# Selective scan: adding sixteen state terms by accumulating transfers into two SBUF sums

## The chip, the cores and the metric

The kernel runs on one core of one Trainium2 chip. The metric is the device time of one execution in microseconds (us). The kernel before takes 5587.63 us, the median of three runs between 5581.73 and 5599.81 us. The profiled execution that this text reads has a span of 5600.4 us. Shares, waits and instants below are of that execution.

## The reference

The program is two layers on an input of 4 images, 128 channels and 64x64 pixels. The first layer is a convolution block with a Mamba (selective scan) branch, the second is attention with 4 heads and a mixture of 8 experts. Only the scan is touched:

```python
dA = jnp.exp(delta[..., None] * A)
dBu = delta[..., None] * Bm[:, :, None, :] * xin[..., None]
def step(h, inp):
    dA_t, dBu_t, C_t = inp
    h = dA_t * h + dBu_t
    y = jnp.einsum('bdn,bn->bd', h, C_t)
    return (h, y)
...
y = jnp.transpose(ys, (1, 0, 2)) + D_skip * xin
out = y * jax.nn.silu(z) @ out_proj_w.T
```

There are N = 16 states for each channel. The einsum is a sum over the 16 states of h times C. It is this sum whose adding changes hands.

## The kernel before

The sequence of each image (4096 positions) is cut into 8 blocks of 512. Channels lie on the 128 partitions, in two halves p = 0 and 1 for each block. One **unit** of the scan is one image, one block, one half and one state: 4 x 8 x 2 x 16 = 1024 units, in that order, one for each turn of the main loop at L1207, called a slot. A unit does the following:

- `fetched` (L732) loads `rows`, B and C of that state broadcast to the partitions, 512 KB, three slots ahead. The pool has four buffers.
- `decayed` (L742) makes `da` = exp(delta x A) on ScalarE, two slots ahead.
- `scan` (L747) runs three VectorE instructions on 128x512 float32: `h` = rows x du, then the scan itself (TENSOR_TENSOR_SCAN, in place in `h`), then `hc` = rows x h, the term of that state. `hc` has 5 buffers (L756).
- ScalarE copies the last column of `h` to `state`, in the next slot.

For the first 128 units (`ALONE`, L1204), when there is no attention to run yet, every term is added by TensorE: a matmul of `hc` with the identity into the PSUM tile `y`. From unit 128 on, GpSimd adds the terms of an even and an odd state in SBUF (L1232), and TensorE adds the eight pair sums into `y` (L1241), two slots later. After the sixteenth state `scanned` (L760) does xin = xin x dsk + y on VectorE, reading PSUM, and zs = xin x zs on GpSimd.

Everything else is woven into the same slots, by two devices. **Attention** is a generator (L894): each slot takes one group, which is four `sc` matmuls, two exponentials `pT` on ScalarE and, a slot later, eight `av` matmul records (`weighted`, L950). Two **lanes**, X and Y, hold generators of stages (group norm, first norm, convolution, the scan's `inputs`, `closed`, and the attention's `finished` with the experts); each half slot moves a lane by one stage. The lanes' layer norms (`normalised`, L502) have a chain of four small GpSimd instructions, `rs` and `shift`, whose result ScalarE needs for `xt` two stages later.

All instructions go through the wrapper at L445, which ties each to the one before it on the same engine. So the order on every engine's queue is the order of this Python text, and an instruction that waits holds back all that are behind it on its engine. For the same reason nearly every row of the profile has line L445, and the tiles' names tell the operations apart. Loads and stores are all issued by SyncE, in one queue.

When the units are used up, near 4976 us, attention groups and the experts remain, up to the end.

Of the kernel before, what the change touches and what calls it, by code (L numbers as in the profile page):

```python
# [9 lines left out]
F32 = mybir.dt.float32  # L10
# [3 lines left out]
ALU = mybir.AluOpType  # L14
# [3 lines left out]
P = 128  # L18
C = 128
EPS = 1e-5  # L20
BLK = 512
# [3 lines left out]
NST = 16  # L25
# [11 lines left out]
def conv_mamba_attn_moe_kernel(ctx: ExitStack, tc: tile.TileContext, t: dict):  # L37
    nc = tc.nc
    x, out = t["x"], t["out"]
# [13 lines left out]
    def load(name, shape=None, src=None, eng=nc.sync, pool=const):  # L53
        src = t[name] if src is None else src
        w = pool.tile(list(shape or src.shape), F32, name=f"w_{name}")
        eng.dma_start(out=w, in_=src)
        return w

    ident = const.tile([P, P], F32, name="ident")
# [13 lines left out]
    inz, cb, dtb, dsk, wbc = (load(k) for k in ("inz", "cb", "dtb", "dsk", "wbc"))  # L73
# [365 lines left out]
    class Queue:  # L439
# [7 lines left out]
    tensor, vector, scalar, gpsimd, sync = (  # L447
        Queue(e) for e in (nc.tensor, nc.vector, nc.scalar, nc.gpsimd, nc.sync)
    )

    def mm(out, lhsT, rhs, start=True, stop=True):
        tensor.matmul(out, lhsT=lhsT, rhs=rhs, start=start, stop=stop)
# [11 lines left out]
    def flush():  # L464
        for entry in outgoing:
            entry[0] -= 1
            if entry[0] == 0:
                sync.dma_start(out=entry[1], in_=entry[2])
        outgoing[:] = [entry for entry in outgoing if entry[0]]
# [7 lines left out]
    def pool(name, bufs=1, space=None):  # L477
        return main.enter_context(
            tc.tile_pool(name=name, bufs=bufs, **({} if space is None else {"space": space}))
        )  # L480

    mix, att, side = pool("mix"), pool("att"), pool("side")
# [48 lines left out]
    group_of, y0_of, xn_of, pairs_of, in_of, gated, kqv = {}, {}, {}, {}, {}, {}, {}  # L531
# [200 lines left out]
    def fetched(b, i, p, n):  # L732

        bcd = in_of[b, i, p][4]
        w = mix.tile([P, 2, BLK], F32, name="rows", bufs=4)
        sync.dma_start(
            out=w.rearrange("p k q -> p (k q)"),
            in_=bcd[:, n, :][None].to_broadcast([DI, 2, 2 * BLK]),
        )
        return w  # L740

    def decayed(b, i, p, n):  # L742
        da = mix.tile([P, BLK], F32, name="da", bufs=3)
        scalar.activation(da, in_of[b, i, p][2], AF.Exp, scale=amat[:, n : n + 1])
        return da

    def scan(b, i, p, n, w, da):  # L747

        du = in_of[b, i, p][3]
        h = mix.tile([P, BLK], F32, name="h", bufs=3)  # L750
        vector.tensor_mul(h, w[:, 0, :], du)
        vector.tensor_tensor_scan(
            out=h, data0=da, data1=h, initial=0.0 if i == 0 else states[b % 2][:, p, n : n + 1],
            op0=ALU.mult, op1=ALU.add,
        )
        hc = mix.tile([P, BLK], F32, name="hc", bufs=5)  # L756
        vector.tensor_mul(hc, w[:, 1, :], h)
        return h, hc

    def scanned(b, i, p, y):  # L760
        xin, zs, delta, du, bcd = in_of.pop((b, i, p))
        vector.scalar_tensor_tensor(xin, xin, dsk, y, ALU.mult, ALU.add)
        gpsimd.tensor_mul(zs, xin, zs)
        gated[b, i, p] = zs

# [184 lines left out]
    def weighted(group):  # L950
        b, q, h, pTs, first, last, prev, final = group
        if first:
            sums[0] = ps_av.tile([P, BLK], F32, name="av")
        av = sums[0]
        for k, (v, pT) in enumerate(pTs):
            for u in range(2):
                mm(
                    av[64 * u : 64 * u + 2 * DH, :], v, pT[:, u, :],
                    first and k == 0, last and k == STEP - 1,
                )  # L960
        if last:
            avs = att.tile([P, BLK], F32, name="avs", bufs=2)
            scalar.copy(avs, av)
            if prev is not None:
                gpsimd.tensor_add(avs, avs, prev)


            if not final:
                partial[b, q, h] = dram.tile([P, BLK], F32, name=f"avd{q}{h}")
                send(partial[b, q, h], avs, 3)  # L970
                return
            if h == 0:
                total[b, q] = dram.tile([2, 2, NH, DH, BLK], F32, name=f"total{q}")
            d = total[b, q]
            send(d[:, :, h].rearrange("u k r q -> (u k) r q"), avs, 3)
            if h == NH - 1:
                work_left = inverted(b, q)
                later.extend((slot + n, work_left) for n in (4, 6, 8))
# [148 lines left out]
    def advance(lane, second):  # L1127

        if inside[lane] != second:
            return False  # L1130
        while True:
            if lane not in running:

                tasks = lanes[lane] if lanes[lane] or slot < len(units) else lanes["X"]
                if not tasks or not all(k in done for k in tasks[0][2]):
                    return False
                key, stages, _ = tasks.popleft()
                running[lane] = key, stages(lane) if callable(stages) else stages
            key, stages = running[lane]
            try:  # L1140
                next(stages)
                inside[lane] = not second
                return True
            except StopIteration:
                assert not second
                done.add(key)
                del running[lane]

    def until(key):
        while key not in done:  # L1150
            flush()
            count = len(done)
            moved = [
                advance(*half) for half in (("X", True), ("Y", False), ("Y", True), ("X", False))
            ]
            assert any(moved) or len(done) > count, key
# [17 lines left out]
    for k in range(-2, len(blocks)):  # L1174
        if 0 <= k:
            b, i = blocks[k]
            Y.append((("in", b, i, 1), inputs(b, i, 1), [("scan", *blocks[k - 1], 1)] if k else []))
        if k + 2 < len(blocks):
            b, i = blocks[k + 2]
            if k + 2 == 0 or i > 0:  # L1180
                upper(k + 2)
        if 0 <= k + 1 < len(blocks):
            b, i = blocks[k + 1]
# [20 lines left out]
    ALONE = NB // 2 * 2 * NST  # L1204
    rows, decays, old, due = {}, {}, None, deque()
    even, y_of, waiting, slot = None, {}, None, 0
    while slot < len(units) or due or waiting or left or later or lanes["X"] or running:  # L1207
        flush()

        for ahead in range(slot if slot == 0 else slot + 3, min(slot + 4, len(units))):  # L1210
            until(("in", *units[ahead][:3]))
            rows[ahead] = fetched(*units[ahead])
        if old:
            (b, i, p, n), h = old
            if i < NB - 1:
                scalar.copy(states[b % 2][:, p, n : n + 1], h[:, BLK - 1 : BLK])
            old = None
        for ahead in range(slot if slot == 0 else slot + 2, min(slot + 3, len(units))):
            decays[ahead] = decayed(*units[ahead])
        group = next(groups, None)  # L1220
        if slot < len(units):
            unit = units[slot]
            h, hc = scan(*unit, rows.pop(slot), decays.pop(slot))
            old = unit, h
            b, i, p, n = unit

            if slot < ALONE:
                due.append((slot + 1, unit, hc, n == 0))
            elif n % 2 == 0:
                even = hc  # L1230
            else:
                gpsimd.tensor_add(even, even, hc)  # L1232
                due.append((slot + 2, unit, even, n == 1))
        advance("X", True)
        advance("Y", False)
        while due and due[0][0] <= slot:
            _, unit, term, first = due.popleft()
            b, i, p, n = unit
            if first:
                y_of[b, i, p] = ps_y.tile([P, BLK], F32, name="y")  # L1240
            mm(y_of[b, i, p], ident, term, first, n == NST - 1)  # L1241
            if n == NST - 1:
                scanned(b, i, p, y_of.pop((b, i, p)))
                done.add(("scan", b, i, p))
                if p == 1:
                    lanes["X"].appendleft((("closed", b, i), closed(b, i), []))
        advance("Y", True)
        if waiting:
            weighted(waiting)
        waiting = group  # L1250
        advance("X", False)
        while later and later[0][0] <= slot:
            next(later.popleft()[1])
        slot += 1
# [6 lines left out]
    with tc.If(nc.values_load(general[0:1, 0:1]) > 0):  # L1261
# [4 lines left out]
        with tc.For_i(0, B, 1) as b:  # L1266
# [3 lines left out]
                out=t_tok.rearrange("p k c -> p (k c)"),  # L1270
                in_=tsave[bass.ds(b, 1)].rearrange("o p q -> (o p) q"),
# [96 lines left out]
```

## Time and profile before

A row is a stretch of the profiled run, with the busy time of each engine as a share of the stretch. The DMA share is the mean busy share of the 16 DMA engines.

| stretch, us | what runs | TensorE | VectorE | ScalarE | GpSimd | DMA |
|---|---|---|---|---|---|---|
| 560 to 4976 | units 128 to 1023, attention, both lanes | 91% | 82% | 75% | 44% | 63% |
| 4976 to 5600 | rest of attention, experts | 92% | 19% | 54% | 7% | 38% |

The first 560 us hold the 128 units without pairing. Instruction times that matter: the pair addition on GpSimd has a mean of 1465 ns (448 of them), a matmul record of `y` 662 ns (1152 of them, two for each matmul), the scan 1464 ns, the two products on VectorE 811 and 783 ns.

How to read it: a busy share says how much room an engine has over the stretch, not which engine sets the pace at an instant. That needs the chain of waits and the timeline, since each engine executes strictly in its own order.

### The profile page before, as it was taken

To read this page: it belongs to the slowest core of one execution; us is meant where nothing else is said; L and a number is where in the kernel's file an instruction comes from. 1 tells how busy PE (TensorE), PEld (TensorE's weight loads), DVE (VectorE), ACT (ScalarE), POOL (GpSimd) and SP (SyncE) were. 2 spreads that over 40 slices of the span, in tenths; PEclk is the share of its full clock that TensorE was granted. 3 is DMA by queue.
4 is the path that set the end of the run, shared out by engine and by line. 5 is a ranking of instruction groups with operands and counts; after the bars stand their busy time and mean duration, and the time that the engine had idled before them with its cause. 6 is when DMAs were issued, how large, how long until landed. Compare 5 with 4: busy or idle time off the path is not lost.

```text
span 5600.4 us, 60586 instructions
## 1 busy us (share of the span) xinstructions
PE 4916.5 (88%) x17866; PEld 2040.8 (36%) x17866; DVE 4174.5 (75%) x6275; ACT 3892.2 (69%) x5957; POOL 2161.8 (39%) x1885
## 2 busy tenths in 40 slices
PE   4666798988999988999998899898999989899997
PEld 2222333333333333333333333333333333344343
DVE  4888877887888888887887888887888888741221
ACT  3455587787777777787777777687777777666553
POOL 2333444454444444445443444444444443320000
PEclk7777799999999999999999999999999999999998
DMA  3455566666666666667665556666765666654432
GB/s 95 169 171 176 194 210 210 205 228 211 230 208 203 210 208 216 205 225 229 224 211 192 192 200 213 219 221 209 232 223 202 206 205 209 210 183 154 147 121 67
DMA packets 427635, 1097.91 MB, mean 196 GB/s; under 512 B 48401, under 2 KB 131746, under 8 KB 427298
## 3 DMA queue, kind: packets, MB, share of 16 engines
q1 hardware_dynamic: 426130, 1093.17, 58.5%
q8 instruction: 144, 2.36, 0.2%
q14 instruction: 193, 1.58, 0.1%
q10 hardware_dynamic: 1168, 0.80, 0.1%
HBM read 941.95 MB, written 135.00 MB: 192 GB/s over the span
## 4 chain that ended last, share of the span: by engine, by line
PE 45%; DVE 21%; ACT 15%; issue 7%; POOL 6%; DMA 5%; SPq 1%; DVEq 0%; ACTq 0%; POOLq 0%
PE av L445 17%; DVE h L445 11%; PE sc L445 10%; PE ps_X L445 8%; PE ps_Y L445 5%; ACT pT L445 5%; PE y L445 4%; ACT L445 3%; ACT xt L445 3%; DVE hc L445 2%; DVE cm L445 2%; POOL rsY L445 1%; POOL rsX L445 1%; DMA ks<-kd 1%; ACT da L445 1%
## 5 line engine op out<-in xcount | busy, mean ns | idle before, releaser
L445 ACT ACTIVATE pT<-sc 128x1024 f32<-128x1024 f32 x2048 | 1983.7, 1022 | 1017.6 <-PE sc L445 1015.2
L445 PE MATMUL av<-pT,v 128*64 128x512 f32 x8192 | 2004.9, 610 | 3.5 <-ACT avs L445 3.3
L445 DVE TENSOR_TENSOR_SCAN h<-da,state,h 128x512 f32<-128x512 f32 x896 | 1311.3, 1464 | 118.6 <-ACT da L445 26.8
L445 PE MATMUL sc<-qs,ks 128*128 128x512 f32 x4096 | 1308.8, 440 | 96.9 <-DMA ks<-kd 51.9
L445 POOL TENSOR_TENSOR hc<-hc 128x512 f32<-128x512 f32 x448 | 655.8, 1465 | 1718.7 <-DVE hc L445 1513.3
L445 PEld LDWEIGHTS sc<-qs,ks 128*128 128x128 f32 x4096 | 717.7, 193 | 773.7 <-ACT pT L445 283.0
L445 PEld LDWEIGHTS av<-pT,v 128*64 128x64 f32 x8192 | 501.6, 137 | 1193.3 <-issue 1105.8
L445 DVE TENSOR_TENSOR h<-rows,du 128x512 f32<-128x512 f32 x1024 | 830.6, 811 | 88.0 <-ACT state L445 38.1
L445 DVE TENSOR_TENSOR hc<-rows,h 128x512 f32<-128x512 f32 x1024 | 802.2, 783 | 78.3 <-DVE h L445 2.3
L445 ACT ACTIVATE da<-delta,amat 128x512 f32<-128x512 f32 x1024 | 749.4, 732 | 9.4 <-DVE h L445 5.2
L445 PE MATMUL y<-hc,ident 128*128 128x512 f32 x1152 | 661.5, 662 | 62.4 <-DVE hc L445 51.3
L445 ACT ACT_TABLE_LOAD x319 | 409.3, 1283 | 22.9 <-PE ps_Y L445 17.8
L445 ACT COPY state<-h 128x1 f32<-128x1 f32 x896 | 175.7, 196 | 194.8 <-DVE h L445 194.3
L445 PEld LDWEIGHTS y<-hc,ident 128*128 128x128 f32 x1152 | 219.6, 209 | 213.8 <-DVE hc L445 101.4
L445 POOL TENSOR_SCALAR rsY<-mvY 128x4 f32<-128x4 f32 x99 | 57.5, 581 | 527.3 <-DVE mvY L445 523.2
L445 POOL TENSOR_TENSOR avs<-avs,prev 128x512 f32<-128x512 f32 x64 | 89.3, 1396 | 438.1 <-ACT avs L445 319.7
L445 PE MATMUL ps_X<-share,w_ew 128*128 128x512 f32 x448 | 223.9, 622 | 20.5 <-DVE share L445 20.2
L445 ACT ACTIVATE xt<-ps_Y,shiftY,rsY 128x128 f32<-128x128 f32 x380 | 143.2, 462 | 129.9 <-POOL shiftY L445 122.4
L445 POOL TENSOR_SCALAR du<-e 128x512 f32<-128x512 f32 x64 | 145.9, 2280 | 217.2 <-ACT e L445 217.2
L445 DVE TENSOR_TENSOR share<-share,xf 128x1024 f32<-128x1024 f32 x128 | 182.8, 1428 | 51.1 <-DMA share<-sharesY 31.0
L445 DVE RECIPROCAL den<-den 128x32 f32<-128x32 f32 x16 | 5.5, 346 | 265.6 <-DMA den<-total 265.6
L445 DVE TENSOR_TENSOR_SCAN h<-da,h 128x512 f32<-128x512 f32 x128 | 182.9, 1429 | 17.3 <-ACT da L445 4.4
(234 smaller groups left out, 4729.6 us busy)
## 6 DMA issues: line engine op xcount, KB each, us to landing
rows<-bcd SPq DMA_DIRECT2D x1024, 512.0 KB
ks<-kd SPq DMA_DIRECT2D x256, 512.0 KB
qs<-qd SPq DMA_DIRECT2D x129, 512.0 KB
v<-vd SPq DMA_DIRECT2D x256, 256.0 KB
share<-sharesX SPq DMA_DIRECT2D x112, 512.0 KB
pairs<-xn SPq DMA_DIRECT2D x128, 128.5 KB
qd<-hi SPq DMA_DIRECT2D x32, 512.0 KB
qd<-lo SPq DMA_DIRECT2D x32, 512.0 KB
```

Of the source, the lines that this page charges most:

```text
L445: return lambda *args, **kw: queued(op(*args, **kw))
```

## The change

From unit 128 on, the terms of states 0 and 1 are written directly to two SBUF tiles, `ysum0` (2 buffers) and `ysum1` (1 buffer). The terms of states 2 to 15 go to `hc` (now 3 buffers) and are added to one of the two tiles by a DMA that GpSimd issues with `accum_op=ALU.add`. Even states and state 15 go to `ysum0`, odd states from 3 to 13 to `ysum1`. After state 15 VectorE folds `ysum1` in with xin x dsk + ysum1, and two slots later adds `ysum0`. The change is meant to free GpSimd and TensorE of the adding. The 128 units of the start stay as they were.

```diff
-        hc = mix.tile([P, BLK], F32, name="hc", bufs=5)
+        if slot >= ALONE and n < 2:
+            hc = mix.tile([P, BLK], F32, name=f"ysum{n}", bufs=2 - n)
+        else:
+            hc = mix.tile([P, BLK], F32, name="hc", bufs=3)
         vector.tensor_mul(hc, w[:, 1, :], h)
...
-        vector.scalar_tensor_tensor(xin, xin, dsk, y, ALU.mult, ALU.add)
+        if isinstance(y, list):
+            vector.tensor_add(xin, xin, y[0])
+        else:
+            vector.scalar_tensor_tensor(xin, xin, dsk, y, ALU.mult, ALU.add)
         gpsimd.tensor_mul(zs, xin, zs)
...
-            elif n % 2 == 0:
-                even = hc
+            elif n < 2:
+                y_of.setdefault((b, i, p), []).append(hc)
             else:
-                gpsimd.tensor_add(even, even, hc)
-                due.append((slot + 2, unit, even, n == 1))
+                to = y_of[b, i, p][n % 2 if n < NST - 1 else 0]
+                gpsimd.dma_start(out=to, in_=hc, accum_op=ALU.add)
+                if n == NST - 1:
+                    xin = in_of[b, i, p][0]
+                    vector.scalar_tensor_tensor(
+                        xin, xin, dsk, y_of[b, i, p][1], ALU.mult, ALU.add
+                    )
+                    due.append((slot + 2, unit, None, False))
...
-            mm(y_of[b, i, p], ident, term, first, n == NST - 1)
+            if term is not None:
+                mm(y_of[b, i, p], ident, term, first, n == NST - 1)
```

## The prediction

> **What bounds the kernel now.** I read the chain of waits first: its summary by engine names no single limit.
>
> ```profile
> PE 45%; DVE 21%; ACT 15%; issue 7%; POOL 6%; DMA 5%; SPq 1%; DVEq 0%; ACTq 0%; POOLq 0%
> ```
>
> TensorE carries less than half of the chain, and VectorE and ScalarE a third. Next, busy time from 560 to 4976 us, the stretch that the change touches (columns: stretch, length, busy us of TensorE, weight loads, VectorE, ScalarE, GpSimd, then clock, DMA share, GB/s).
>
> ```profile
> 560.00:4976.00 4416.00, 3998.62 (x14826) 1658.84 (x14826) 3640.45 (x5280) 3299.82 (x5072) 1940.76 (x1637) 0.96 0.63 212
> ```
>
> TensorE is busy 91% and VectorE 82%; the DMA engines have 37% left. The 624 us after it and the 560 us before it run the same instructions after the change. Third, the timeline of plain slots, in which no lane adds work (start, duration, engine, operation).
>
> ```profile
> 2402.60 1.19 PE L445 MATMUL sc<-qs,ks 128*128 128x512 f32 x4
> 2403.63 1.02 PE L445 MATMUL y<-hc,ident 128*128 128x512 f32 x2
> 2404.58 1.94 PE L445 MATMUL av<-pT,v 128*64 128x512 f32 x8
> 2406.45 1.19 PE L445 MATMUL sc<-qs,ks 128*128 128x512 f32 x4
> 2407.57 1.94 PE L445 MATMUL av<-pT,v 128*64 128x512 f32 x8
> 2409.44 1.20 PE L445 MATMUL sc<-qs,ks 128*128 128x512 f32 x4
> ```
>
> TensorE runs without a gap. A slot with a `y` matmul lasts 3.85 us (2402.60 to 2406.45), one without it 2.99 us (to 2409.44): the matmul costs 0.86 us. VectorE in the same place, with the GpSimd addition:
>
> ```profile
> 2406.55 1.28 DVE L445 TENSOR_TENSOR_SCAN h<-da,state,h 128x512 f32<-128x512 f32 x1
> 2407.94 0.69 DVE L445 TENSOR_TENSOR hc<-rows,h 128x512 f32<-128x512 f32 x1
> 2408.55 0.69 DVE L445 TENSOR_TENSOR h<-rows,du 128x512 f32<-128x512 f32 x1
> 2409.34 2.13 DVE L445 TENSOR_TENSOR_SCAN h<-da,state,h 128x512 f32<-128x512 f32 x1
> ...
> 2408.71 1.68 POOL L445 TENSOR_TENSOR hc<-hc 128x512 f32<-128x512 f32 x1 [4.74 <-DVE hc L445]
> ```
>
> The scan takes 1.28 us alone and 2.13 us when it comes up while GpSimd adds. So the addition, on an engine that is 44% busy, costs VectorE up to 0.85 us in every second slot.
>
> [...]
>
> **The change part by part.** In 896 units there are 896/16 = 56 sums, with 14 accumulating transfers each: 784 of 256 KB.
>
> *TensorE.* 448 `y` matmuls go: 448 x 0.86 = 385 us, the ceiling of the gain where TensorE sets the pace. On the chain, asked for 600 to 4976 us alone, `PE y` has 4.6%: 0.046 x 4376 = 201 us.
>
> *VectorE.* 448 GpSimd additions go. At most each releases 0.85 us: 381 us. For the lower end: by the tile views the medians of scan, first and second product are 1284, 684 and 692 ns against means of 1464, 811 and 783 ns, so collisions with all of GpSimd cost 896 x 0.180 + 1024 x 0.127 + 1024 x 0.091 = 384 us; the additions are 653 of GpSimd's 1941 us in this stretch, which gives 0.34 x 384 = 130 us. I take 230 us. VectorE is a fifth of the chain, 927 us, so 230/3640 of that is 58 us on the path. Added are 56 `tensor_add` of 0.69 us, 39 us, a fifth of it on the path: 8 us. The fold with dsk moves two slots ahead and reads SBUF; it costs what it did.
>
> *Mechanism alone:* 201 + 58 - 8 = about 250 us.
>
> *GpSimd.* It loses 656 us of additions and issues 784 transfers. An issue costs 0.52 us on SyncE (the median of the `rows` issues)[...]. I take 1 us: 784 us, about what goes, so its load stays as it is. Its queue is what matters: each transfer waits for `hc` and for the previous transfer into the same sum, two slots back (at state 15, one slot back). Behind it stand the `rs` and `shift` chain, for which ScalarE's `xt` waits with `pT` queued behind that, and `du`, `delta` and `zs`. VectorE's `hc` waits for the transfer three back (3 buffers).
>
> *Latency L of one transfer, from issue to landing.* [...] High end: a 256 KB load on SyncE's queue, `inv`, took 9.49 us on the chain at 1368 us with other loads ahead of it. The transfers have a queue of their own beside SyncE's[...]. I take 6 us. What does L do? From the timeline I took the starts of all GpSimd pair additions: 440 gaps, mean 9.96, median 9.5, a quarter under 7.55 us. Take 0.86 us off every gap and let none be under L: the sum of the changes is -369 us at L = 4, -307 at 6, -200 at 7, -45 at 8, +165 at 9, +298 at 9.5, +442 at 10. So L = 6 takes back 369 - 307 = 62 us, and the change breaks even near 8.2 us.
>
> *DMA engines.* By the queue table 1093.17 MB take 58.5% of 5600 us, 3276 us: 256 KB are 0.79 us of all 16 engines. With one read the transfers add 784 x 0.79 = 616 us, with two 1232 us, to 0.63 x 4416 = 2782 us: a share of 77 to 91%. Loads come later then. Waits on loads are now 5% of the chain, 220 us in this stretch; I let them grow by a quarter, 55 us.
>
> *Sum:* -250 + 62 + 55 = -133 us, so 5588 - 133 = 5455; I say **5460 us**. Costed at nothing: freed PSUM use, and the wait of VectorE for `y` (71 us in this stretch), which the wait for state 15's transfer replaces. That one ends 2L = 12 us after state 14's product and is needed three slots (14.8 us at 4.93 each) after it.
>
> **The rivals.**
> - *Cheap transfers.* One read and L under 5 us: the stretch gains nearly the whole mechanism, 250 us: 5340 us. For it: 37% of the DMA engines is idle. [...]
> - *A wash.* DMA delays eat the gain: 5590 us.
> - *The DMA engines become the bound.* With two reads, 2782 + 1232 = 4014 us of work; if they reach 89% at most, the stretch lasts 4510 us, 94 longer: 5680 us. For it: SyncE's loads come in bursts (five behind each other at 1368 us), and a wait for `ks` stops TensorE and ScalarE together. Against: the loads are issued two to three slots ahead.
> - *The chain of transfers is the bound.* L of 9.5 us: +298, so 5885 us; slower than before. For it: the 9.49 us seen. Against: that load stood behind others in its own queue.
>
> **How the numbers follow.** Forecast 0.44, cheap transfers 0.13, wash 0.08, DMA engines 0.18, chain of transfers 0.17. Faster 0.57, same 0.08, slower 0.35. The range of 5300 to 5850 us reaches past cheap transfers and the DMA bound, and holds of the last rival what lies under L = 9.4; about 0.17 is left out.
>
> **What would show it.** In the changed kernel's profile: `y` matmuls near 256 records instead of 1152; slots without lane work near 3.0 us in the timeline; the scan's mean down from 1464 towards 1350 ns; GpSimd waiting on DMA for little; DMA share 0.75 to 0.9 with waits for `ks` and `rows` under twice theirs. The forecast is wrong if `xt` or `hc` waits long for GpSimd or for the transfers (L over 8 us), or if TensorE idles on `ks`.

## The result, and the profile after

The changed kernel takes 5774.87 us, the median of four runs (5763.86 to 5780.07); the kernel before took 5589.66 us beside it. The ratio is 1.0328 (95% interval 1.0303 to 1.0352): 3.3% slower, where 5460 us had been forecast. Since the comparison with each experiment has runs of the kernel before on the same chip, whose medians lie between 5589 and 5593 us, medians are compared directly below, and each verdict has its ratio. The runs of one kernel spread over 10 to 40 us, so a single difference of 20 us or less between two medians says little.

The loss lies in the stretch that the change touches. Same columns as before, from 560 us to the last unit of the scan:

```profile
560.00:5128.00 4568.00, 3758.78 (x13869) 1551.27 (x13869) 3488.02 (x5323) 3291.47 (x5057) 1916.28 (x1967) 0.91 0.87 248
```

The last `rows` load is issued at 5127.9 us instead of 4954.1, so the stretch has grown by 174 us, although up to these instants TensorE (first busy column) is busy 218 us less than before (3976.7 us then) and VectorE (third) 141 us less (3628.5). The DMA share rose from 0.63 to 0.87. TensorE's granted clock fell from 0.96 to 0.91. The page's chain, its queues and the transfers' row:

```profile
q1 hardware_dynamic: 426130, 1093.17, 57.1%
q0 software_dynamic: 112896, 205.57, 20.0%
...
PE 31%; DVE 21%; DMA 18%; ACT 13%; POOL 8%; issue 7%; SPq 1%; DVEq 0%; POOLq 0%; ACTq 0%
...
L445 POOL DMA_DIRECT2D ysum<-hc x784 | 694.7, 896 | 2072.2 <-DVE hc L445 1051.9
...
ysum<-hc POOLq DMA_DIRECT2D x784, 256.0 KB, 7.0
```

The chain went from TensorE (45% to 31%) to DMA (5% to 18%). `q0` is the new queue: 205.57 MB cost a fifth of the 16 engines, while `q1` moves five times the bytes for 57.1%. An issue occupies GpSimd for 896 ns on average, so 784 of them take 694.7 us, and a transfer lands 7.0 us after its issue (last column, the median). The waits say who pays (engine and tile, what it waited for: us in total, times, longest):

```profile
POOL ysum L445 <- DMA ysum<-hc: 495.0, 128, 9.5
ACT xt L445 <- POOL shiftY L445: 186.2, 70, 24.6
DVE xin L445 <- DMA ysum<-hc: 149.0, 53, 10.0
PE sc L445 <- DMA ks<-kd: 89.9, 16, 16.6
DVE h L445 <- DMA rows<-bcd: 68.9, 31, 7.1
```

GpSimd waits 495 us for the previous transfer into the same sum, VectorE 149 us at the folds. ScalarE's `xt` waits 186.2 us for GpSimd's `shiftY` instead of 122.4. But loads that have nothing to do with the sums are waited for longer too: `ks` 89.9 us against 51.9 before, `rows` 68.9 against 20.1. Which of these sets the time can't be read from totals of waits. That is what the experiments are for.

### The profile page after: what moved, and what is told of

Its sections match the earlier page's. It is cut to its first block, busy times and chain, and to the rows that moved or that the text cites. A ratio compares the mean times of both kernels' runs of the same rounds, so it can differ in the third digit from the quotient of the medians.

```text
span 5778.0 us, 59802 instructions
## 1 busy us (share of the span) xinstructions
PE 4694.6 (81%) x16970; PEld 1941.2 (34%) x16970; DVE 4034.7 (70%) x6331; ACT 3896.3 (67%) x5957; POOL 2143.3 (37%) x2221
## 3 DMA queue, kind: packets, MB, share of 16 engines
q1 hardware_dynamic: 426130, 1093.17, 57.1%
q0 software_dynamic: 112896, 205.57, 20.0%
## 4 chain that ended last, share of the span: by engine, by line
PE 31%; DVE 21%; DMA 18%; ACT 13%; POOL 8%; issue 7%; SPq 1%; DVEq 0%; POOLq 0%; ACTq 0%
PE av L445 11%; DVE h L445 11%; DMA ysum<-hc 8%; PE ps_X L445 7%; PE sc L445 7%; PE ps_Y L445 5%; ACT pT L445 4%; ACT xt L445 2%; ACT L445 2%; DMA inv<-inverse 2%; POOL rsY L445 2%; DVE hc L445 2%; POOL rsX L445 2%; DVE cm L445 2%; DMA pairs<-xn 2%
## 5 line engine op out<-in xcount | busy, mean ns | idle before, releaser
L445 PE MATMUL av<-pT,v 128*64 128x512 f32 x8192 | 2082.6, 631 | 8.6 <-ACT avs L445 8.5
L445 PE MATMUL sc<-qs,ks 128*128 128x512 f32 x4096 | 1348.7, 451 | 164.6 <-DMA ks<-kd 89.9
L445 POOL DMA_DIRECT2D ysum<-hc x784 | 694.7, 896 | 2072.2 <-DVE hc L445 1051.9
L445 DVE TENSOR_TENSOR_SCAN h<-da,state,h 128x512 f32<-128x512 f32 x896 | 1235.6, 1379 | 118.3 <-ACT da L445 25.9
L445 DVE TENSOR_TENSOR h<-rows,du 128x512 f32<-128x512 f32 x1024 | 810.4, 791 | 132.5 <-DMA rows<-bcd 68.9
L445 DVE TENSOR_TENSOR hc<-rows,h 128x512 f32<-128x512 f32 x912 | 705.2, 773 | 98.5 <-DMA ysum<-hc 61.9
L445 ACT ACTIVATE xt<-ps_Y,shiftY,rsY 128x128 f32<-128x128 f32 x380 | 143.2, 459 | 194.3 <-POOL shiftY L445 186.2
L445 PE MATMUL ps_X<-ident,xt 128*128 128x128 f32 x372 | 105.7, 349 | 194.2 <-ACT xt L445 182.4
L445 POOL TENSOR_TENSOR zs<-xin,zs 128x512 f32<-128x512 f32 x64 | 105.4, 1646 | 327.1 <-DVE xin L445 327.1
L445 PE MATMUL y<-hc,ident 128*128 128x512 f32 x256 | 176.2, 792 | 51.3 <-DVE hc L445 51.3
L445 PE MATMUL ps_Y<-ident,xt 128*128 128x128 f32 x396 | 82.6, 343 | 157.7 <-ACT xt L445 157.3
L445 PE MATMUL ps_Y<-pairs,inxc 128*128 128x512 f32 x256 | 147.1, 704 | 63.1 <-DMA pairs<-xn 57.8
```

Source lines behind the costliest of these rows:

```text
L445: return lambda *args, **kw: queued(op(*args, **kw))
```

## The experiments

Two theories stood at the start. **Latency:** engines wait for transfers to land. **Load:** the transfers fill the DMA engines and everybody's loads come late. A third possibility was that taking the adders off is worth less than thought.

### No transfers at all

```diff
-                gpsimd.dma_start(out=to, in_=hc, accum_op=ALU.add)
```

> The changed kernel without its 784 accumulating transfers: the terms of states 2 to 15 are computed but left out of the sums, everything else stays. It measures what taking the adding off GpSimd and TensorE is worth when nothing replaces it. Theory of latency (engines wait for the landing of transfers) and theory of load (the transfers fill the DMA engines and SyncE's loads come late) both expect the whole mechanism of the prediction, some 250 us under the kernel before: 5340 us, 5280 to 5400. A theory that the mechanism itself is small (other engines take over at once) expects 5500 us or more.

Measured: 5424.89 us, ratio 0.9699 (0.9678 to 0.9720). The mechanism is worth 166 us, two thirds of the forecast's 250, and the transfers with all that hangs on them cost 5775 - 5425 = 350 us.

### The same load, with nobody waiting

```diff
+    spare = [mix.tile([P, BLK], F32, name=f"spare{k}") for k in range(3)]
...
-                to = y_of[b, i, p][n % 2 if n < NST - 1 else 0]
+                to = spare[n % 3]
...
-                        xin, xin, dsk, y_of[b, i, p][1], ALU.mult, ALU.add
+                        xin, xin, dsk, fixed, ALU.mult, ALU.add
```

The terms of states 0 and 1 go to `hc` here, like the others, and the second fold reads `fixed` (a constant tile) too.

> The same 784 accumulating transfers of 256 KB, issued at the same places, but into three rotating spare tiles that nobody reads, so that each waits for the transfer three slots back instead of two or one, and the folds on VectorE read a constant tile and wait for no transfer (the terms of all states are left out of the sums). DMA load and issue stay as in the changed kernel. Theory of load: about as slow as the changed kernel, 5700 to 5780 us, DMA share 0.87. Theory of latency: close to the kernel without transfers, 5340 to 5420 us.

Measured: 5668.29 us, ratio 1.0126 (1.0104 to 1.0148). Of the 350 us, 243 remain when no fold waits for a transfer and no transfer waits for a recent one. So waiting for the sums isn't the whole cost, and load isn't either: it leaves 107 us unexplained. The 243 us aren't load alone. They hold the issues on GpSimd, which are measured further below, and VectorE still waits 46.3 us at `hc` for the transfer three back, because `hc` has three buffers. Three rows of its waits for loads:

```profile
DVE h L445 <- DMA rows<-bcd: 113.1, 38, 8.4
PE sc L445 <- DMA ks<-kd: 108.2, 17, 16.2
PE ps_Y L445 <- DMA pairs<-xn: 72.7, 21, 11.4
```

All three are loads of SyncE's queue; without transfers these waits are 37.2, 58.2 and 30.2 us. Nothing in this kernel ties the loads to the sums, so the shared DMA engines, of which the two queues take 58.3% and 20.3% here, are the likely reason. This is argued: no view here gives the landing time of each load.

### Half the bytes, and plain copies

```diff
-                gpsimd.dma_start(out=to, in_=hc, accum_op=ALU.add)
+                gpsimd.dma_start(out=to[:, 0 : BLK // 2], in_=hc[:, 0 : BLK // 2], accum_op=ALU.add)
```

> The changed kernel with transfers of columns 0 to 255 only (128 KB instead of 256 KB; the other half of each term is left out of the sums). Number of issues and all waits stay. Both theories expect a gain; load: about half of what the transfers cost, near 5550 us, DMA share about 0.76, transfers landing in some 5 us instead of 7.0. Latency: more than half, since 5 us is under the two slots of most pairs: 5450 us or less.

Measured: 5626.03 us, ratio 1.0054 (1.0037 to 1.0071). Both expectations missed. 5550 us fit a kernel without transfers at 5340 us, as it was expected then; with the measured 5425 us, half of the cost recovered would be 5600 us. Half the bytes recover 149 of the 350 us, a little under half. These transfers land in 5.8 us, against 7.0 at full width and some 5 expected. The tiny transfers below show better that a part of the cost goes with the number of transfers and not with their size.

```diff
-                gpsimd.dma_start(out=to, in_=hc, accum_op=ALU.add)
+                gpsimd.dma_start(out=to, in_=hc)
```

> The changed kernel with plain copies in place of accumulating transfers: same bytes written, same queue, same waits, but the old sum isn't read (the sums then hold only the last term). If accumulating makes a transfer dear by its second read, the software queue falls from 20% of the DMA engines to about 10%, the landing from 7.0 to 5 to 6 us, and the time to near that of the half-width transfers, 5550 us. If a 2 KB row from GpSimd's queue is dear in any case, it stays at 5750 us and 20%.

Measured: 5591.22 us, ratio 1.0002 (0.9987 to 1.0017), 184 us under the changed kernel. The rows of the queue, of the issues and of the transfers in this kernel, in turn:

```profile
q0 software_dynamic: 62720, 205.57, 9.4%
...
L445 POOL DMA_DIRECT2D ysum<-hc x784 | 439.8, 561 | 2026.7 <-DVE hc L445 1363.9
...
ysum<-hc POOLq DMA_DIRECT2D x784, 256.0 KB, 5.4
```

The same 205.57 MB take 9.4% of the engines instead of 20.0%, with 62720 packets instead of 112896, which is 64 fewer for each transfer, and land in 5.4 us instead of 7.0. The issue on GpSimd also fell, from 896 to 561 ns. So accumulating doubles the time that a transfer takes of the DMA engines, as the forecast's upper end had it. Queue and landing are as the first branch expected, the time is 41 us above it. The 184 us are the price of accumulating as a whole: shorter issues and shorter waits at the folds (70.6 us) are in it, beside the load.

### Tiny transfers, with and without the folds' wait

```diff
-                gpsimd.dma_start(out=to, in_=hc, accum_op=ALU.add)
+                gpsimd.dma_start(out=to[:, 0:8], in_=hc[:, 0:8], accum_op=ALU.add)
```

> The changed kernel with transfers of 8 columns (4 KB in all; the other 504 columns of each term are left out of the sums). 784 issues on GpSimd and every wait stay; hardly any load is left. If load explains what the transfers cost (243 of 350 us by the three rotating tiles), this lands near the kernel without transfers, 5425 us plus the issues: 5440 to 5490 us. If the count of transfers, their issue on GpSimd and the waits on a landing[...] matter most, 5530 us or more.

Measured: 5525.41 us, ratio 0.9870 (0.9849 to 0.9892). With 4 KB for each transfer 100 of the 350 us remain. The next kernel has the same transfers and folds that read the constant tile:

> The 8-column transfers with the two folds on VectorE reading a constant tile (the scan's output leaves out all terms from unit 128 on). It splits the 100 us between no transfers (5425) and 8-column transfers (5525). If VectorE's wait at the folds is the cost, 5450 us; if it is the 784 issues of 0.9 us on GpSimd, which hold back rs and shift and with them ScalarE's xt, 5510 us.

Measured: 5506.26 us, ratio 0.9845 (0.9828 to 0.9861). Only 19 us of the 100 are the folds' wait; 81 us stay with transfers that hardly carry anything and that VectorE's folds ignore. The tiny transfers' time to landing, from the answer for their tile:

```profile
DMA to landing us min/median/max: 2.0/4.7/9.3
```

Even 4 KB take 4.7 us in the median, beside a fastest of 2.0 us. The same 4 KB can land in 2.0 us, so more than half of the median is waiting of some kind; what it waits for isn't shown.

### What the issues on GpSimd cost

The 81 us had been costed at nothing. Two kernels without transfers put something else in their place:

```diff
-                gpsimd.dma_start(out=to, in_=hc, accum_op=ALU.add)
+                gpsimd.memset(spare, 0.0)
+                gpsimd.memset(spare, 0.0)
```

> The kernel without transfers (the terms of states 2 to 15 left out of the sums) with two memsets of a spare 128x512 tile on GpSimd in the place of each transfer, some 0.4 to 0.5 us each, that wait for no other engine; hc has 2 buffers. If the time that GpSimd is occupied by the issues is their cost, 5500 us, as with tiny transfers that nobody waits for (5506). If it is the wait for hc or the transfers themselves, 5430 us.

Measured: 5465.14 us, ratio 0.9770 (0.9753 to 0.9787): 40 us over the kernel without transfers. The second kernel waits, but does little:

```diff
-                gpsimd.dma_start(out=to, in_=hc, accum_op=ALU.add)
+                gpsimd.tensor_copy(spare, hc[:, 0:1])
```

> The kernel without transfers (the terms of states 2 to 15 left out of the sums) with a GpSimd copy of one column of hc in the place of each transfer: GpSimd's queue waits for every hc as in the changed kernel, but is occupied for a short time only. If the wait in the in-order queue holds back rs and shift, 5490 us or more. If occupation is the cost, 5430 to 5445 us.

Measured: 5441.53 us, ratio 0.9719 (0.9694 to 0.9743): 17 us, of the size of the interval. The rows of the two replacements, in turn:

```profile
L445 POOL MEMSET spare<- 128x512 f32 x1568 | 824.8, 526 | 71.9
```

```profile
L445 POOL COPY spare<-hc 128x1 f32<-128x1 f32 x784 | 317.1, 405 | 1845.5 <-DVE hc L445 1818.8
```

At 526 ns each the memsets kept GpSimd busy longer than the issues would (824.8 us against 694 us) and cost half of the 81 us. The copies occupy GpSimd too, for 317.1 us, so the two experiments overlap: occupation and the in-order wait for `hc` explain at most 57 of the 81 us. The rest is left to what the tiny transfers do beyond that (their waits on each other, 206 us on GpSimd, and their 112896 packets). No run takes it apart.

### The folds' wait at full size

The changed kernel, with both folds reading the constant tile:

> The changed kernel in which the two folds on VectorE at the end of each sum read a constant tile in place of ysum (so the scan's output leaves out all terms); the transfers, their load and their waits on each other stay. VectorE then waits for a transfer at hc alone. Of the 107 us between the changed kernel (5775) and the three rotating tiles (5668): if VectorE's wait for state 15's transfer is the cost, about 5690 us; if GpSimd's wait for the transfer two slots or one slot back is, with rs and shift behind it, about 5760 us.

Measured: 5689.13 us, ratio 1.0180 (1.0157 to 1.0202), 86 us under the changed kernel. It is VectorE's wait at the folds that costs, and not GpSimd's far longer wait for its own chain, which is still 447.6 us here: against the rotating tiles (5668 us), the chained transfers cost 21 us. The chain of waits of the changed kernel shows one such fold (start, length, what):

```profile
2826.18 7.87 DMA ysum<-hc
2834.05 0.02 issue
2834.07 0.02 POOLq L445
2834.09 0.49 issue
2834.59 7.63 DMA ysum<-hc
2842.22 0.02 issue
2842.24 0.04 DVE xin L445
```

State 14's transfer lands at 2834.05, state 15's is issued only then into the same sum, and lands at 2842.22. Two landings in a row take 16 us, and VectorE stands still for the last 2.48 us of it, with the next `h`, scan and `hc` behind (they start at 2842.85, 2843.64 and 2845.77 us). The fold in the timeline:

```profile
2842.24 0.69 DVE L445 TENSOR_TENSOR xin<-xin,ysum 128x512 f32<-128x512 f32 x1 [2.48 <-DMA ysum<-hc]
```

The next kernel gives the last fold one slot more:

```diff
-                    due.append((slot + 2, unit, None, False))
+                    due.append((slot + 3, unit, None, False))
```

> The changed kernel with the last fold (tensor_add of ysum0) three slots after state 15's transfer instead of two; nothing is left out. If that wait of VectorE is what the fold costs (86 us by the constant fold), the time falls to some 5710 us; if the sum's later end holds back the next block's inputs as much as the wait did, it stays at 5775 us.

Measured: 5701.66 us, ratio 1.0198 (1.0180 to 1.0217). One slot more gives back 73 of the 86 us; the later end of the sum costs little. VectorE's wait at the folds falls from 149.0 to 78.7 us:

```profile
DVE xin L445 <- DMA ysum<-hc: 78.7, 38, 9.5
```

### The mechanism, split

```diff
-                gpsimd.tensor_add(even, even, hc)
```

> The kernel before without the 448 additions on GpSimd, the matmuls of y stay (the odd terms from unit 128 on are left out of the sums). It splits the 166 us that the kernel without transfers gained. The prediction gave VectorE's relief 58 us on the path, so 5530 us; if the collisions of VectorE with GpSimd were under-rated, 5480 us; if they lie beside the path, 5575 us or more.

Measured: 5508.01 us, ratio 0.9850 (0.9834 to 0.9867): 83 us for GpSimd's additions. VectorE's busy time falls by 211 us (4174.5 to 3963.1).

```diff
-            mm(y_of[b, i, p], ident, term, first, n == NST - 1)
+            if slot < ALONE + 1:
+                mm(y_of[b, i, p], ident, term, first, n == NST - 1)
+            elif first:
+                mm(y_of[b, i, p], ident, term, True, True)
```

> The kernel before with the GpSimd additions, but of the eight matmuls of each sum from unit 128 on only the first stays, 392 fewer (seven of eight pair sums are left out). The prediction gave TensorE's relief 201 us on the path for 448, so 176 us here: 5415 us. If ScalarE and VectorE take over at once, or TensorE's clock falls[...], 5480 to 5540 us.

Measured: 5521.62 us, ratio 0.9870 (0.9853 to 0.9886): 70 us for 392 matmuls, which is 80 us for 448. 83 + 80 = 163 us agrees with the 166 us of taking away both. 5521.62 us lie in the range that was set for other engines taking over or a falling clock. Busy times by engine, before and without these matmuls:

```profile
PE 4916.5 (88%) x17866; PEld 2040.8 (36%) x17866; DVE 4174.5 (75%) x6275; ACT 3892.2 (69%) x5957; POOL 2161.8 (39%) x1885
```

```profile
PE 4668.4 (85%) x17082; PEld 1932.7 (35%) x17082; DVE 4194.5 (76%) x6275; ACT 3886.8 (70%) x5957; POOL 2183.6 (40%) x1885
```

The `y` records alone fell by 422 us (661.5 to 239.2), but TensorE as a whole by 248 us. 77 us of the difference are `av` and `sc`, whose records grew longer; the granted clock of the whole run went from 0.944 to 0.923. The page's chain by engine, first without the additions, then without the matmuls:

```profile
PE 50%; ACT 17%; DVE 17%; issue 5%; DMA 5%; POOL 5%; SPq 1%; DVEq 0%; ACTq 0%; POOLq 0%
```

```profile
PE 36%; DVE 27%; ACT 15%; POOL 7%; issue 7%; DMA 6%; SPq 1%; DVEq 0%; ACTq 0%; POOLq 0%
```

So the clock fell, and other engines took over as well. Each relief moves the chain onto the other engine: VectorE goes from 21% to 27% as soon as the matmuls are gone, and TensorE from 45% to 50% without the additions.

### Two other ways to add

```diff
-                gpsimd.tensor_add(even, even, hc)
-                due.append((slot + 2, unit, even, n == 1))
+                gpsimd.dma_start(out=even, in_=hc, accum_op=ALU.add)
+                due.append((slot + 3, unit, even, n == 1))
```

> The kernel before with each GpSimd pair addition replaced by one accumulating transfer of the odd term into the even one; TensorE adds the pair sums as before, one slot later, hc has 6 buffers. 448 transfers, none of which waits for another. Theory of load, in proportion: 5508 us without additions plus 243 x 448/784 = 139, so 5647 us. If only chained transfers are dear, 5530 us, under the kernel before.

Measured: 5632.17 us, ratio 1.0076 (1.0059 to 1.0093). The proportional estimate of 5647 us holds within 15 us. With six buffers VectorE waits only 12.8 us at `hc` here, so the wait for an `hc` buffer isn't what makes the transfers dear in this kernel. Transfers that wait for no other one still cost more than the GpSimd additions they replace.

```diff
-            if slot < ALONE:
+            if slot < len(units):
```

> The kernel before with every term added by TensorE, one slot after it is made, as the first 128 units do: 448 more matmuls of y, no GpSimd additions, no transfers. By what the first 448 cost (5508 against 5425, 83 us) this would be 5591 us, even with the kernel before. If TensorE, 91% busy already, then sets the pace alone, 0.86 us each: 5890 us.

Measured: 5670.74 us, ratio 1.0134 (1.0117 to 1.0151), between the two expectations. On TensorE the first 448 matmuls cost 83 us (5508 against 5425), the next 448 cost 163 us:

```profile
PE 66%; DVE 11%; ACT 10%; DMA 4%; POOL 4%; issue 4%; SPq 1%; DVEq 0%; ACTq 0%; POOLq 0%
```

The kernel before stands between two engines: it takes half of the matmuls away from TensorE at the price of 83 us on GpSimd and VectorE. None of the complete ways to add that were run beats it.

## Why the prediction was wrong

The pieces, from experiment to experiment, in the order of the sum: 5591 - 166 (adders gone) + 81 (tiny transfers, folds not waiting) + 183 (5689 - 5506, full size) + 86 (folds waiting) = 5775 us. The forecast's sum had -250, 0, and 62 + 55 = 117 for the last two. Beside 3 us in the start, the 320 us between its 5455 and the 5775 us are 84 us too much relief, 81 us of issues, and 152 us too little for load and landing together. The split of the pieces holds for this order of taking things away. Of the signs that the forecast named, the 256 `y` records, slots of 3.0 us, a DMA share of 0.87 and `ks` waits under twice theirs came true (for the slots: `sc` starts at 2832.60 and 2835.59 us in the changed kernel); GpSimd waited 495 us for transfers instead of little, and waits for `rows` grew 3.4 times.

- **TensorE, mis-sized.** The step "on the chain `PE y` has 4.6%: 201 us" took the share of one row on the chain for what its removal brings. Measured 80 us. The slots without lane work did go to 3.0 us, as foretold. Around them VectorE took over part of the chain (21% to 27%), and TensorE's other matmuls grew longer as its clock fell (a record of `av` from 610 to 624 ns, the clock from 0.944 to 0.923, with 392 of the matmuls gone). How much of the missing 121 us goes to each stays open. A share on a chain doesn't say what stands just behind it, and the forecast counted all of it.
- **VectorE, of the right order.** The relief was sized well: 230 us taken, 211 measured in busy time, with the scan's mean at 1379 ns against a foretold 1350. The 58 us on the path can't be tested apart: the 83 us hold everything that hangs on GpSimd's additions, and 825 us of memsets on GpSimd cost 40 us with no addition there. That GpSimd's own time counts, the forecast had left out.
- **GpSimd's issues, costed at nothing.** The duration was good (1 us taken, 0.9 measured), and "its load stays as it is" held too: 695 us of issues for 656 us of additions. The fault was to call that free. The additions cost 83 us in their place, and the issues, with tiny transfers and all that these do, 81 us.
- **Latency.** The 6 us, like the 1 us of an issue, were the author's estimate: GpSimd issues no transfer in the kernel before, so no trace of it could show either. Measured were 7.0 us against these 6. By the forecast's own table that is worth 107 us more. But the table applied one floor to all pairs, and by the experiments the price was paid mainly at one place, so that the table's 107 us and the measured 86 + 21 = 107 us agree by luck: the step "costed at nothing: the wait of VectorE for `y`, which the wait for state 15's transfer replaces" failed. It set 2L = 12 us against three mean slots, 14.8 us. Worked out from the timeline of all 56 sums, VectorE was ready for the last fold 14.2 us after the end of state 14's product in the mean, so the slots were right. In 32 sums it had to wait; in these the transfer of state 15 landed 16.3 us after that product and VectorE was ready after 12.8 us (17.2 and 14.7 us in the sum shown). So the landings were mis-sized, and means left no room for their scatter. It cost 86 us.
- **DMA engines, under-sized.** The share of 0.87 was inside the foretold 0.77 to 0.91. Its upper end took the price of two reads for an accumulating transfer. That was the author's assumption: the trace doesn't show reads apart from writes. The measured price, 20.0% of the engines against 9.4% for plain copies, is of that size. What failed is "I let them grow by a quarter, 55 us": the step from tiny to full transfers cost 183 us. Some 21 us of these are the chained waits on GpSimd, by the rotating tiles; these tiles, with no chain and no fold waiting, stand 162 us above the tiny transfers (5668 - 5506). Between these two kernels the waits for `rows`, `ks` and `pairs` grew at unchanged loads, from 39.3, 58.0 and 30.7 us to 113.1, 108.2 and 72.7 us. That loads and transfers wait for each other in the engines is the author's reading of it, and isn't shown. VectorE's wait at `hc` (12.9 to 46.3 us between these two kernels) is in the 162 us as well.
- **The rivals.** The rival in which the DMA engines become the bound came nearest in cause, but said 5680 us. Its 4510 us for 4014 us of DMA work are a share of 0.89, which was assumed; 0.87 was measured. With the 86 us at the folds, which it had left out, it would have said 5766 us; that this is near the measured time is luck in part, since it counted neither the relief nor the issues.

The issues on GpSimd don't show in VectorE's scans as the additions did: the mean of a scan is 1376 ns with 784 tiny transfers and 1378 ns with none, against 1464 ns in the kernel before and 1380 ns there without its additions. For the product `h` it is open, since that mean is 780 ns with the tiny transfers (folds not waiting) and 759 ns with none.

## What to carry to other kernels

An accumulating transfer is not a free adder: here it took twice the engine time of a plain copy (20.0% against 9.4%), its issues occupied GpSimd as long as the additions that they spared (695 us for 656), and it landed after 7.0 us, which a chain of sums adds up. Before moving work to the DMA engines, price the loads that are already there at the new share, and find the one place where a compute engine in strict order must wait for the last landing, with the scatter of landings and slots and not their means. When a kernel stands between two engines, what removing work from one of them brings is measured by leaving that work out, and not by its share on the chain.

## What the runs showed of the hardware that was not expected

After the longer of its waits for `ks` TensorE worked more slowly for some microseconds, so a late load can be paid for twice. The timeline of the changed kernel, TensorE alone:

```profile
4085.19 2.03 PE L445 MATMUL sc<-qs,ks 128*128 128x512 f32 x4 [3.31 <-DMA ks<-kd]
4087.15 2.64 PE L445 MATMUL av<-pT,v 128*64 128x512 f32 x8
4089.73 1.21 PE L445 MATMUL sc<-qs,ks 128*128 128x512 f32 x4
4090.85 0.66 PE L445 MATMUL ps_Y<-ident,xt 128*128 128x128 f32 x4
4091.43 1.94 PE L445 MATMUL av<-pT,v 128*64 128x512 f32 x8
```

After a wait of 3.31 us for `ks` the four `sc` matmuls take 2.03 us instead of 1.21, and the eight `av` 2.64 instead of 1.94; 4.5 us after the first of them `sc` is back at 1.21. So it had about 60% of its rate (1.21 over 2.03) after the wait. Of the 16 waits for `ks` in this execution, ten of 2.77 to 16.64 us are followed by four `sc` in 2.03 to 2.07 us, one of 2.66 us by 1.67 us, and five of 0.16 to 1.96 us by 1.15 to 1.38 us.

The clock also bears on the mechanism. The mean `av` record rose from 610 to 624 ns when 392 matmuls of `y` were left out, and to 622 ns in the kernel without transfers, where 448 are gone; without the GpSimd additions alone it stayed at 609 ns. The granted clock of the whole run was 0.944 before, 0.923 and 0.928 in the first two of these, 0.950 in the third, and 0.959 with every term added by TensorE. From 560 us to about the end of the scan TensorE's busy share and clock are, in order: 82% and 0.91 in the changed kernel, 86% and 0.94 without the matmuls, 87% and 0.94 without transfers, 91% and 0.96 before, 92% and 0.97 without the additions, 96% and 0.98 with every term on TensorE. So in these runs the clock followed TensorE's work, and part of what taking work off it gains was given back. In the changed kernel the `av` and `sc` records together are busy 118 us longer than before (2082.6 + 1348.7 against 2004.9 + 1308.8). How much of that lies on the path, no run here separates.
